# Layer 0 of a graph-attention network: logits with neighbours on partitions, block sums moved behind their transposes, and a new order for the opening turn

## The chip, the cores and the metric

The kernel runs on 1 core of one Trainium2 chip. The metric is the device time of one execution in microseconds (us). Before the change the median of 3 runs is 3023.37 us (3021.89 to 3024.65). TensorE is called PE here, VectorE DVE, ScalarE ACT, GpSimd POOL; SP is the engine that issues all DMAs of this kernel.

## The reference

Two layers work on x of 128 graphs with 64 nodes and 768 features, all in float32. This is layer 0 with its residual and norm, which the change touches (12 heads of 64):

```
h    = einsum('bnd,ade->bane', x, W);  th = tanh(h)
attn = (th @ w_src) + swapaxes(th @ w_dst, 2, 3)        # [b, a, n, m]
attn = where(attn >= 0, attn, 0.2 * attn)
attn = where(~adj, -999.0, attn);  attn = softmax(attn, axis=-1)
f    = elu(einsum('banm,bame->bane', attn, h) + b)
gate = sigmoid(x @ H_w.T + H_b)
x1   = layernorm(x + gate * f + (1 - gate) * x)
```

Layer 1 is a 6-head attention on x1 (q, k, v, an adjacency mask, an output product, residual, norm). Its value product v = x1 @ Wv is computed in the first stage together with layer 0.

## The kernel before

**Tiles.** 64 tiles of 128 tokens (two graphs each) are taken in 32 pairs. A product of a pair (256 x 768 by 768 x 768) is done with seven half-size products instead of eight (Strassen-Winograd), numbered 1 to 7; each is six matmuls 128 x 384. The input side needs four block sums of each operand: `weight_sums` for a weight, `block_sums` for x (`x_sums`, on POOL) and for x1 (`v_sums`, on DVE). A `Job` (L150 to L198) holds the two accumulators of one product, y and z. Products 1, 6, 7 and 4 accumulate in the same y bank, 5 and 3 in the same z bank, so each has to wait until the result before it was read out of the bank (`way_out`).

**Turns.** The first stage is one loop over p (L563), 34 turns. Turn p computes the h and gate products of pair p ("h", "g"), and the attention, norm and value product of pair p-1 ("v", and "u" for the two last v products, which fall into the turn after). `TURN` (L52) is the order of the 21 products in a turn, positions 0 to 20. All other work is hung on these positions by hand, with `at(pos, ...)` (L584 to L614). [...] A product's way out is emitted after the next product (`step`, L208), or at once where the position holds no product (`flush`).

**One tile's attention.** `products` takes tanh of h (ACT) and multiplies by w_dst (DVE) and w_src (POOL); `terms` reduces both (DVE), sends the dst terms to DRAM, waits on SP for their landing, and loads them back spread over partitions as `dd`; `with_bias` adds the bias to h (POOL) and makes `hx`, h with the two graphs of a tile swapped. `logits` adds source and dst terms (DVE), `leaky` applies the slope (ACT), `masked` writes -999 by a predicate, takes the row maximum and subtracts it (DVE), `exps` takes exp (ACT). Now nodes n are on partitions and neighbours m are on the free axis, so `probs_by_nodes` turns the probabilities with six PE transposes per tile, and ACT copies the result `pT` out of PSUM. `attend` multiplies by h (24 matmuls 64 x 64 x 66 on PE, with a column of ones that gives the softmax denominator), `features` divides (DVE) and takes exp for elu (ACT), `elu1`, `gated` (DVE) and `residual` (POOL) form x1, `stats` and `normed` normalise it (DVE, one POOL power, ACT), `by_features` turns it with six PE transposes into `x1T`, which the v product takes. Transposes and attends share two PSUM banks, tag "m" (L95).

In the turn of pair p, `t1`, `t0` are the two tiles of pair p-1 and `n1`, `n0` those of pair p; n1 of one turn is t1 of the next.

**The opening.** All weights are loaded by SP in one row of DMAs, with the sums of w0 and wv on DVE and those of the gate weight on POOL (L262 to L278).

**The second stage** (layer 1, from L629) is not changed, except that a call now reads `all_of(...)`.

Of the kernel before, what the change touches and what calls it, by code (L numbers as in the profile page):

```python
# [9 lines left out]
F32 = mybir.dt.float32  # L10
U8 = mybir.dt.uint8
# [17 lines left out]
NEG0 = -999.0  # L29
# [21 lines left out]

TURN = [  # L52
# [6 lines left out]
def kernel(  # L59
# [4 lines left out]
    adj: bass.AP,  # L64
    w0: bass.AP,
# [36 lines left out]
    dst_d = [dram.tile([P, H0], F32, name=f"dstd_{t}") for t in range(2 * NP)]  # L102
# [10 lines left out]
    neg0 = const.tile([P, 1], F32, name="neg0")  # L113
    V.memset(neg0, NEG0)

# [5 lines left out]
    def load_weight(src, tag, name):  # L121

        w = wpool.tile([P, 7, HK, HALF], F32, tag=tag, name=name)
        view = src.rearrange("(kh kc p) (nh f) -> kh nh p kc f", p=P, kc=HK, nh=2)
        for block, kh, nh in ((B11, 0, 0), (B21, 1, 0), (B22, 1, 1), (T3, 0, 1)):
            nc.sync.dma_start(out=w[:, block], in_=view[kh, nh])
        return w

    def weight_sums(eng, w):
        eng.tensor_tensor(w[:, T1], w[:, T3], w[:, B11], ALU.subtract)  # L130
        eng.tensor_tensor(w[:, T2], w[:, B22], w[:, T1], ALU.subtract)  # L131
        eng.tensor_tensor(w[:, T4], w[:, B21], w[:, T2], ALU.subtract)
        eng.tensor_tensor(w[:, T3], w[:, B22], w[:, T3], ALU.subtract)
# [102 lines left out]
    with ExitStack() as ph:  # L236
# [7 lines left out]
        def load_xT(p):  # L244
            t = sb.tile([P, KC, PAIR * P], F32, tag="xT", name=f"xT_{p}")
            nc.sync.dma_start(out=t, in_=xT[p])
            return t
# [14 lines left out]
        xTs = {0: load_xT(0)}  # L262
# [9 lines left out]
        for s in x_steps:  # L272
            s()
        weight_sums(V, w0_w)
        weight_sums(G, hw_w)
        V.tensor_scalar(b01_bc, b01_bc, 1.0, None, ALU.add)
        wv_w = load_weight(wv, "wc", "wv")
        weight_sums(V, wv_w)  # L278

        def work(name):  # L280
            return sb.tile([P, D], F32, tag="work", name=name, bufs=5)
# [81 lines left out]
        def terms(t):  # L363

            th = st[t].pop("th")
            sd = small.tile([P, 2 * H0], F32, tag="sd", name=f"sd_{t}")
            V.tensor_reduce(sd, th.rearrange("p s (a e) -> p (s a) e", e=E0), AX.X, ALU.add)
            st[t]["sd"] = sd
            nc.sync.dma_start(out=dst_d[t], in_=sd[:, :H0])
            dd = work(f"dd_{t}")  # L370
            for g in range(2):
                nc.sync.dma_start(
                    out=dd[g * N : (g + 1) * N, :],
                    in_=dst_d[t][g * N : (g + 1) * N, :]
                    .rearrange("m a -> (m a)")
                    .partition_broadcast(N),
                )
            st[t]["dd"] = dd

        def with_bias(t):  # L380

            h = st[t]["h"]
            G.tensor_tensor(
                h[:, :, :E0], h[:, :, :E0], b01_bc.unsqueeze(1).to_broadcast([P, H0, E0]), ALU.add
            )

            hx = sb.tile([P, J0, EP], F32, tag="hx", name=f"hx_{t}")
            nc.sync.dma_start(out=hx[:N], in_=h[N:, :J0, :])
            nc.sync.dma_start(out=hx[N:], in_=h[:N, J0:, :])
            st[t]["hx"] = hx  # L390

        def logits(t):
            sd, dd = st[t].pop("sd"), st[t].pop("dd")
            att = work(f"att_{t}")
            att3 = att.rearrange("p (a m) -> p a m", m=N)
            V.tensor_tensor(
                att3,
                dd.rearrange("p (m a) -> p a m", a=H0),
                sd[:, H0:].unsqueeze(2).to_broadcast([P, H0, N]),
                ALU.add,  # L400
            )
            st[t]["att"] = att

        def leaky(t):
            att = st[t]["att"]
            S.activation(att, att, AF.Prelu, alpha=LEAKY)

        def masked(t):

            att = st[t]["att"]  # L410
            att3 = att.rearrange("p (a m) -> p a m", m=N)
            V.copy_predicated(
                att3,
                st[t]["nadj"].unsqueeze(1).to_broadcast([P, H0, N]),
                neg0.unsqueeze(1).to_broadcast([P, H0, N]),
            )
            mx = small.tile([P, H0], F32, tag="mx", name=f"mx_{t}")
            V.tensor_reduce(mx, att3, AX.X, ALU.max)
            V.tensor_tensor(att3, att3, mx.unsqueeze(2).to_broadcast([P, H0, N]), ALU.subtract)

        def exps(t):

            att = st[t].pop("att")
            prob = work(f"prob_{t}")
            S.activation(
                prob.rearrange("p (j a m) -> p a j m", a=2, m=N),
                att.rearrange("p (a j m) -> p a j m", a=2, m=N),
                AF.Exp,
            )
            st[t]["prob"] = prob  # L430
# [8 lines left out]
        def probs_by_nodes(t):  # L439
            prob = st[t].pop("prob")  # L440
            pT = sb.tile([P, J0, P], F32, tag="pT", name=f"pT_{t}", bufs=1)
            for half in range(2):
                transposed(
                    pT[:, 3 * half : 3 * half + 3, :],
                    prob[:, half * HALF : (half + 1) * HALF],
                    f"pTp_{t}_{half}",
                )
            st[t]["pT"] = pT

        def attend(t):  # L450
            pT, h, hx = st[t].pop("pT"), st[t].pop("h"), st[t].pop("hx")
            av = [bank("m", f"av_{t}_{a}") for a in range(2)]
            for j in range(J0):
                for a in range(2):
                    rows = slice(a * N, (a + 1) * N)
                    for g in range(2):
                        T.matmul(
                            av[a][g * N : (g + 1) * N, j * EP : (j + 1) * EP],
                            pT[rows, j, g * N : (g + 1) * N],
                            h[rows, a * J0 + j, :] if a == g else hx[rows, j, :],  # L460
                            start=True,
                            stop=True,
                        )
            st[t]["av"] = av
# [62 lines left out]
        def mask(p):  # L527
            ad = load_adj(sb, 2 * p, PAIR, f"adj_{p}")
            na = sb.tile([P, PAIR, N], U8, tag="nadj", name=f"nadj_{p}", bufs=2)
            V.tensor_scalar(na, ad, 0, None, ALU.is_equal)  # L530
            for i in range(PAIR):
                st[2 * p + i]["nadj"] = na[:, i, :]
# [23 lines left out]
        def x_sums(p):  # L556
            A[p], steps = sums_of(G, "sx", xTs[p], f"x{p}")
            for s in steps:
                s()
# [3 lines left out]
        for p in range(NP + 2):  # L563
# [8 lines left out]
            def at(pos, ok, *acts):  # L572
                if ok:
                    plan.setdefault(pos, []).extend(acts)

            def do(f, *args):
                return lambda: f(*args)
# [4 lines left out]


            at(0, old, do(probs_by_nodes, t1), do(exps, t0), do(gate_tanh, t1))  # L584
            at(1, old, do(residual, t1))
            at(2, old, do(attend, t1), do(gate_tanh, t0))
            at(3, old, do(features, t1), do(probs_by_nodes, t0), do(residual, t0))
            at(4, old, do(elu1, t1), do(gated, t1))
            at(5, old, do(attend, t0), do(stats, t1))
            at(6, old, do(features, t0), do(normed, t1))  # L590
            at(7, old, do(elu1, t0), do(gated, t0))
            at(8, old, do(by_features, t1), do(stats, t0))
            at(9, old, do(normed, t0))
            at(12, old, do(v_begins))
            at(15, old, lambda: v_sums[q][0](), lambda: v_sums[q][1](), do(spill_features, q))
# [8 lines left out]
            at(11, old, do(by_features, t0))  # L604
# [4 lines left out]
            at(16, new, do(logits, n1))  # L609
            at(17, new, do(leaky, n1))  # L610
            at(17, p + 1 < NP, do(x_sums, p + 1))
            at(18, new, do(masked, n1), do(logits, n0))
            at(19, new, do(exps, n1), do(leaky, n0))
            at(20, new, do(masked, n0))  # L614

            for pos, (job, i) in enumerate(TURN):
                ok = {"h": new, "g": new, "v": old, "u": 0 <= p - 2 < NP}[job]
                if ok:
                    step(jobs["u" if job == "u" else job], int(i))
                else:  # L620
                    flush()
                for act in plan.get(pos, ()):
                    act()
# [5 lines left out]
    with ExitStack() as ph:  # L629
# [24 lines left out]
        weight_sums(V, wq_w)  # L654
        loaded = load_group(0)
        wk_w = load_weight(wk, "wb", "wk")
        weight_sums(V, wk_w)
        wf_w = load_weight(wf, "wc", "wf")
        weight_sums(V, wf_w)
# [260 lines left out]
```

## Time and profile before

The profiled execution took 3022.04 us of device time; its span from the first to the last instruction is 3020.0 us, and 2.04 us lie around it.

| what | number |
|---|---|
| median of 3 runs | 3023.37 us |
| profiled execution, its span | 3022.04 us, 3020.0 us |
| mean granted TensorE clock | 0.986 |
| opening until the second turn's first product | 0 to 51.8 us |
| first stage, steady turns | 45.6 us each |
| last product of the first stage ends, layer 1's first starts | 1515 us, 1532.5 us |

In the groups, a line is that of a helper where one records all products (L173). "[idle <- X]" is the time that the engine stood idle before an instruction, and what ended it. "DMA issue" is the time on SP; the landing comes later.

### The profile page before, as it was taken

To read this page: it belongs to the slowest core of one execution; us is meant where nothing else is said; L and a number is where in the kernel's file an instruction comes from. 1 tells how busy PE (TensorE), PEld (TensorE's weight loads), DVE (VectorE), ACT (ScalarE), POOL (GpSimd) and SP (SyncE) were. 2 spreads that over 40 slices of the span, in tenths; PEclk is the share of its full clock that TensorE was granted. 3 is DMA by queue.
4 is the path that set the end of the run, shared out by engine and by line. 5 is a ranking of instruction groups with operands and counts; after the bars stand their busy time and mean duration, and the time that the engine had idled before them with its cause. 6 is when DMAs were issued, how large, how long until landed. Compare 5 with 4: busy or idle time off the path is not lost. (4 is left out here: it accounts for less than half of the span.)

```text
span 3020.0 us, 45321 instructions
## 1 busy us (share of the span) xinstructions
PE 2931.3 (97%) x18048; PEld 2029.7 (67%) x18048; DVE 1830.8 (61%) x3017; ACT 1006.5 (33%) x1761; POOL 805.5 (27%) x650
## 2 busy tenths in 40 slices
PE   6999999999999999999869999999999999999997
PEld 3666666666666666666558777787777787777784
DVE  5888888888888888888633344434344434344434
ACT  2444344344444444444412222222222222222221
POOL 4324324324323333333212111211211211211211
PEclk8999999999999999999879999999999999999998
DMA  4333333333333333333242111222111222111211
GB/s 168 115 112 109 116 118 107 112 120 112 108 121 114 109 117 119 107 113 114 90 146 86 62 57 58 85 85 79 62 57 57 85 85 79 62 57 57 85 64 63
DMA packets 174929, 284.81 MB, mean 94 GB/s; under 512 B 46208, under 2 KB 112768, under 8 KB 174720
## 3 DMA queue, kind: packets, MB, share of 16 engines
q1 hardware_dynamic: 174720, 281.92, 28.7%
q8 instruction: 143, 2.34, 0.3%
q14 instruction: 66, 0.54, 0.1%
HBM read 167.81 MB, written 101.06 MB: 89 GB/s over the span
## 5 line engine op out<-in xcount | busy, mean ns | idle before, releaser
L487 POOL TENSOR_TENSOR x<-gate,x 128x768 f32<-128x768 f32 x64 | 116.5, 1821 | 330.9 <-ACT gate L538 330.9
L780 POOL TENSOR_TENSOR y<-y,bf_bc 128x768 f32<-128x768 f32 x64 | 114.3, 1816 | 301.7 <-DMA y<-x1d 301.7
L804 DVE TENSOR_TENSOR y<-y_o,y 128x384 f32<-128x384 f32 x128 | 69.8, 553 | 178.0 <-PE y_o L173 171.0
L222 POOL TENSOR_TENSOR rs_b<-ve_b,minus_half 128x1 f32<-128x1 f32 x64 | 35.1, 549 | 483.6 <-DVE ve_b L220 480.7
L675 DVE TENSOR_TENSOR kT<-z_k,kT 128x256 f32<-128x256 f32 x96 | 40.5, 422 | 203.6 <-ACT kT L674 108.9
L173 PE MATMUL y_q<-a,wq 128*128 128x256 f32 x576 | 141.7, 382 | 17.4 <-DMA a<-x1Td 17.4
L360 POOL TENSOR_TENSOR th<-th,wsd 128x768 f32<-128x768 f32 x64 | 116.0, 1812 | 157.5 <-DVE th L359 157.5
L143 POOL TENSOR_TENSOR sq_q<-a,a 128x768 f32<-128x768 f32 x16 | 29.5, 1844 | 466.6 <-PE y_o L173 311.0
L674 ACT ACTIVATE qT<-y_q,bq_c 128x256 f32<-128x256 f32 x144 | 67.3, 468 | 244.6 <-PE y_q L173 222.8
L173 PE MATMUL y_k<-a,wk 128*128 128x256 f32 x576 | 144.9, 388 | 1.8 <-DMA wk<-in_wk_dram 1.8
L173 PE MATMUL y_g<-hw,sx_x 128*128 128x384 f32 x384 | 136.0, 491 | 10.5 <-DVE gate L336 10.5
L173 PE MATMUL z_k<-sq_q,wk 128*128 128x256 f32 x576 | 141.5, 382 | 4.1 <-DVE qT L675 4.1
L173 PE MATMUL y_o<-wf,so_o 128*128 128x384 f32 x384 | 134.4, 494 | 8.8 <-DVE y L804 8.8
L173 PE MATMUL y_h<-w,xT 128*128 128x384 f32 x384 | 136.3, 492 | 6.8 <-DMA w<-in_w_dram 6.8
L173 PE MATMUL y_k<-sq_q,wk 128*128 128x256 f32 x576 | 141.5, 382 | 0.7 <-DVE wk L131 0.7
L173 PE MATMUL y_q<-sq_q,wq 128*128 128x256 f32 x576 | 140.0, 379 | 0.0
L173 PE MATMUL z_q<-sq_q,wq 128*128 128x256 f32 x576 | 140.0, 379 | 0.0
L222 POOL TENSOR_TENSOR rs_a<-ve_a,minus_half 128x1 f32<-128x1 f32 x64 | 35.2, 551 | 383.9 <-DVE ve_a L220 383.9
L173 PE MATMUL z_v<-wv,sv_v 128*128 128x384 f32 x384 | 137.5, 495 | 0.1
L173 PE MATMUL z_h<-w,sx_x 128*128 128x384 f32 x384 | 137.6, 495 | 0.0
L173 PE MATMUL y_h<-w,sx_x 128*128 128x384 f32 x384 | 135.5, 490 | 1.7 <-DVE w L131 1.7
L173 PE MATMUL y_v<-wv,x1T 128*128 128x384 f32 x384 | 136.5, 492 | 0.6 <-ACT v L349 0.6
(163 smaller groups left out, 6718.7 us busy)
## 6 DMA issues: line engine op xcount, KB each, us to landing
xT<-in_xT_dram SPq DMA_DIRECT2D x32, 768.0 KB, 7.0
x<-in_x_dram SPq DMA_DIRECT2D x64, 384.0 KB, 3.5
dd<-dstd SPq DMA_DIRECT2D x128, 192.0 KB, 3.4
x1d<-x SPq DMA_DIRECT2D x64, 384.0 KB, 2.5
x1Td<-x1T SPq DMA_DIRECT2D x32, 768.0 KB, 4.8
vd<-v SPq DMA_DIRECT2D x64, 384.0 KB, 2.9
a<-x1Td SPq DMA_DIRECT2D x64, 384.0 KB, 3.3
v<-vd SPq DMA_DIRECT2D x384, 64.0 KB, 2.3
```

The source lines that it names most:

```text
L143: lambda: eng.tensor_tensor(s1, a21, a22, ALU.add),
L173: T.matmul(to[:, : self.n], lhsT, rhs, start=kc == 0 and not more, stop=kc == HK - 1, skip_group_check=more,)
L222: G.tensor_tensor(rstd, ve, minus_half, ALU.pow)
L360: G.tensor_tensor(th[:, 1, :], th[:, 1, :], wsd[:, 1, :], ALU.mult)
L487: G.tensor_tensor(xp, st[t]["gate"], xp, ALU.mult)
L674: lambda mn, bk_: S.activation(at(*mn), bk_, AF.Identity, bias=bias(mn[1])),
L675: lambda mn, bk_: V.tensor_tensor(at(*mn), bk_, at(*mn), ALU.add),
L780: G.tensor_tensor(y[:, i, :], y[:, i, :], bf_bc, ALU.add)
L804: V.tensor_tensor(at(*mn), b, at(*mn), ALU.add)
```

## The change

It has five parts.

1. **Logits transposed.** The source terms, not the dst terms, go through DRAM and come back as `ss`, spread so that a partition is a neighbour m and the free axis is (n, head). The own term of the second half of the heads has to come from the tile's other graph, which two small DMAs bring (`dx`). The mask becomes a cap, `cap` (-300 for no edge, 1e30 for an edge), on a transposed copy of the adjacency that the host prepares (`adjT`), and the logits take the minimum with it. The row maximum and its subtraction go. `exps` writes `pT` directly, with a step of 64 elements. `probs_by_nodes` goes, with its 12 transposes a turn and the copies of ACT.
2. **Positions.** `attend` and everything after it moves one to three positions earlier, the logits of n1 and n0 one later (17, 19), `gate_tanh` and `residual` of the first tile into the turn before (19, 20).
3. **x1 sums.** `by_features` of t0 moves from 11 to 10; the first two `v_sums` from 15 to 11, ahead of `products`.
4. **The opening.** Turn 0 runs all h products, then all gate products (`FIRST`), with every way out at once. A weight's third block to load is now T3, then B22. The sums of wv are spread over turn 1.
5. **Small.** `work` has 4 buffers for 5, `pT` 2 for 1; the bias's +1 goes to POOL; the first xT is loaded in two parts.

```diff
-NEG0 = -999.0
+NEG0 = -300.0
+BIG = 1e30
+FIRST = ["h1", "h2", "h6", "h5", "h7", "h4", "h3", "g1", "g2", "g6", "g5", "g7", "g4", "g3"]
+FIRST_AT = {11: 7, 12: 8, 13: 9, 14: 10, 15: 11, 17: 12, 18: 13, 19: 13, 20: 13}
...
-        for block, kh, nh in ((B11, 0, 0), (B21, 1, 0), (B22, 1, 1), (T3, 0, 1)):
+        for block, kh, nh in ((B11, 0, 0), (B21, 1, 0), (T3, 0, 1), (B22, 1, 1)):
...
-        V.tensor_scalar(b01_bc, b01_bc, 1.0, None, ALU.add)
+        G.tensor_scalar(b01_bc, b01_bc, 1.0, None, ALU.add)
         wv_w = load_weight(wv, "wc", "wv")
-        weight_sums(V, wv_w)
...
-            nc.sync.dma_start(out=dst_d[t], in_=sd[:, :H0])
-            dd = work(f"dd_{t}")
-            for g in range(2):
...
+            nc.sync.dma_start(
+                out=src_d[t].rearrange("(a g) (n j) -> (g n) a j", a=2, j=J0),
+                in_=sd[:, H0:].rearrange("p (a j) -> p a j", j=J0),
+            )
+            ss = work(f"ss_{t}")
+            for r in range(2):
+                rows = src_d[t][0:4:3, :] if r == 0 else src_d[t][1:3, :]
+                nc.sync.dma_start(
+                    out=ss[r * N : (r + 1) * N, :].rearrange("p (a x) -> p a x", a=2),
+                    in_=rows.partition_broadcast(N),
+                )
+            dx = small.tile([P, J0], F32, tag="dx", name=f"dx_{t}")
+            nc.sync.dma_start(out=dx[:N], in_=sd[N:, J0:H0])
+            nc.sync.dma_start(out=dx[N:], in_=sd[:N, J0:H0])
...
-            V.tensor_tensor(
-                att3,
-                dd.rearrange("p (m a) -> p a m", a=H0),
...
+            for a, d in ((0, sd[:, :J0]), (1, dx)):
+                half = slice(a * HALF, (a + 1) * HALF)
+                V.tensor_tensor(
+                    att[:, half].rearrange("p (n j) -> p n j", j=J0),
+                    ss[:, half].rearrange("p (n j) -> p n j", j=J0),
+                    d.unsqueeze(1).to_broadcast([P, N, J0]),
+                    ALU.add,
+                )
             V.tensor_tensor(
+                att.rearrange("p (x j) -> p x j", j=J0),
+                att.rearrange("p (x j) -> p x j", j=J0),
+                st[t]["cap"].unsqueeze(2).to_broadcast([P, 2 * N, J0]),
+                ALU.min,
             )
...
-            V.copy_predicated(
...
-            V.tensor_reduce(mx, att3, AX.X, ALU.max)
-            V.tensor_tensor(att3, att3, mx.unsqueeze(2).to_broadcast([P, H0, N]), ALU.subtract)
...
+        def probs(t):
             S.activation(att, att, AF.Prelu, alpha=LEAKY)
+            pT = sb.tile([P, 2, J0, N], F32, tag="pT", name=f"pT_{t}")
             S.activation(
+                pT.rearrange("p a j n -> p a n j"),
+                att.rearrange("p (a n j) -> p a n j", a=2, j=J0),
                 AF.Exp,
             )
...
-        def probs_by_nodes(t):
...
             for j in range(J0):
                 for a in range(2):
                     for g in range(2):
+                        r = g if a == 0 else 1 - g
+                        rows = slice(r * N, (r + 1) * N)
...
-                            pT[rows, j, g * N : (g + 1) * N],
-                            h[rows, a * J0 + j, :] if a == g else hx[rows, j, :],
+                            pT[rows, a, j, :],
+                            h[rows, j, :] if a == 0 else hx[rows, j, :],
...
+            cap = sb.tile([P, PAIR, 2 * N], F32, tag="cap", name=f"cap_{p}")
+            V.tensor_scalar(cap, ad, BIG, NEG0, ALU.mult, ALU.add)
...
-            at(0, old, do(probs_by_nodes, t1), do(exps, t0), do(gate_tanh, t1))
-            at(1, old, do(residual, t1))
-            at(2, old, do(attend, t1), do(gate_tanh, t0))
-            at(3, old, do(features, t1), do(probs_by_nodes, t0), do(residual, t0))
-            at(4, old, do(elu1, t1), do(gated, t1))
-            at(5, old, do(attend, t0), do(stats, t1))
-            at(6, old, do(features, t0), do(normed, t1))
-            at(7, old, do(elu1, t0), do(gated, t0))
-            at(8, old, do(by_features, t1), do(stats, t0))
-            at(9, old, do(normed, t0))
-            at(12, old, do(v_begins))
-            at(15, old, lambda: v_sums[q][0](), lambda: v_sums[q][1](), do(spill_features, q))
+            at(0, old, do(probs, t0), do(gate_tanh, t0))
+            at(1, old, do(residual, t0))
+            at(1, old, do(attend, t1))
+            at(2, old, do(features, t1))
+            at(3, old, do(attend, t0), do(elu1, t1), do(gated, t1))
+            at(4, old, do(features, t0), do(stats, t1))
+            at(5, old, do(elu1, t0), do(gated, t0))
+            at(6, old, do(normed, t1), do(stats, t0))
+            at(8, old, do(by_features, t1), do(normed, t0))
+            at(10, old, do(by_features, t0))
+            at(11, old, do(v_begins), lambda: v_sums[q][0](), lambda: v_sums[q][1]())
+            at(15, old, do(spill_features, q))
...
-            at(11, old, do(by_features, t0))
...
-            at(16, new, do(logits, n1))
-            at(17, new, do(leaky, n1))
+            at(17, new, do(logits, n1))
             at(17, p + 1 < NP, do(x_sums, p + 1))
-            at(18, new, do(masked, n1), do(logits, n0))
-            at(19, new, do(exps, n1), do(leaky, n0))
-            at(20, new, do(masked, n0))
+            at(18, new, do(probs, n1))
+            at(19, new, do(logits, n0), do(gate_tanh, n1))
+            at(20, new, do(residual, n1))
...
+            if p == 1:
+                for pos, s in zip((0, 2, 4, 6), weight_sums(V, wv_w)):
+                    at(pos, True, s)
+            for pos, (job, i) in enumerate(TURN if p > 0 else FIRST):
...
```

## The prediction

> **What bounds the kernel now.** I read first the engines' shares and the slices by time, then three steady turns by window, then the order in time of one turn, and last who waits for whom in the steady part.
>
> ```profile
> PE   6999999999999999999869999999999999999997
> DVE  5888888888888888888633344434344434344434
> PEclk8999999999999999999879999999999999999998
> ```
> The first 19 slices (75.5 us each) are the first stage. PE is full there but for the first slice.
>
> ```profile
> 790.40:836.00 45.60, 45.60 (x248) 27.71 (x247) 37.91 (x55) 19.94 (x33) 16.52 (x14) 1.00 0.35 113
> 836.00:881.60 45.60, 45.60 (x248) 27.72 (x247) 37.90 (x55) 19.93 (x33) 16.52 (x14) 1.00 0.36 117
> ```
> The columns are the window, then busy PE, weight loads, DVE, ACT, POOL, the clock, DMA. A turn is 45.60 us of PE with no gap; DVE has 37.9. So PE work that goes is time saved, until something else comes late.
>
> ```profile
> 835.98 2.10 PE L173 MATMUL y_h<-w,xT 128*128 128x384 f32 x6
> 837.91 0.82 PE L436 MATMUL pTp<-ident,prob 128*128 128x128 f32 x6
> 838.57 2.10 PE L173 MATMUL x_h<-w,xT 128*128 128x384 f32 x6
> ```
> A product takes 1.936 us from start to start, this group of six transposes 838.57 - 837.91 = 0.66; the other, behind an attend, 0.78 (in the last full turn, 1438.20 to the next product at 1438.98). Together 1.44 us a turn.
>
> What comes next behind PE is the turn's own latency:
>
> ```profile
> 809.36 1.01 ACT L226 ACTIVATE x<-x,sh_a,rs_a 128x768 f32<-128x768 f32 x1
> 811.37 0.82 PE L436 MATMUL x1Tp<-ident,x 128*128 128x128 f32 x6
> ```
> x1 of t1 is normed at 810.37, and PE turns it at 811.37: 1.0 us in hand. That is less than the 1.44 the change takes from PE.
>
> **What the Trainium skill says.** "TensorE: Matmul & The Clock Gate", section PE-mode transpose, gives about 275 ns for a transpose in a kernel; the trace has the same mean (280), but queued behind each other six take 0.66 us, 0.11 each, so the sum uses that. "SBUF — State Buffer", section Who interferes with whom: a DVE instruction with two SBUF inputs and a POOL instruction that reads SBUF lock each other out for a whole instruction. The trace agrees for the lock, on a tensor-scalar, which the page also names:
>
> ```profile
> 845.44 1.82 POOL L487 TENSOR_TENSOR x<-gate,x 128x768 f32<-128x768 f32 x1 [0.16 <-ACT gate L538]
> 845.64 1.70 DVE L530 TENSOR_SCALAR nadj<-adj 128x128 uint8<-128x128 uint8 x1
> ```
> The mask took 0.21 us at 34.1 alone, here 1.70, until POOL ended. The same page, section Door 1: The DMA port swizzle, has a penalty for steps beyond 16 bytes; the logits' add, which reads `dd` at 48 bytes, has a least time of 1.52 us against 0.96 for other adds of that size, which agrees. "DMA: Bandwidth & Descriptors", Specifications, says that pieces under 512 B cost a read-modify-write; the dst terms (48 B pieces) landed after 1.4 us at least, and no row separates this.
>
> **The change, part by part.** *Transposes*: 2 x 6 a turn, minus 1.44 us of PE, if nothing comes late; the four ACT copies behind them (0.48 us each) go too, off the path. The attend's 24 matmuls keep number and size, and their order still alternates quadrants: 0. *DVE per tile*: out go 1.89 (add), 1.09 (predicated copy), 0.95 (max), 0.96 (subtraction); in come two adds of 384 (0.56 each by rows of that size) and a minimum of 768 (0.96): 2.0 us from start to end. DVE drops by about 2 x 2.8 = 5.6 to 32 us of a 44.2 us turn, so it is no bound by busy time. The mask doubles its elements: 0.2 to 0.3 us.
>
> *The chain of waits of a turn.* I time from T, the end of product h4 (815.90 here). E, the start of the next turn, is T + 20.1 before and after.
> - Terms of n1. Before, the dst DMA is issued at 822.85, T + 6.95. `by_features` t0 now stands ahead of it: on ACT two copies (0.86) come ahead of the copy of h4 and the tanh, and the second tanh product waits for POOL's lock. I get +1.1: T + 8.0. The two sums themselves are not what is waited for (the first needs only t1, the second the first copy of t0).
> - SP. In order it has src n1, ss, ss, dx, dx, hx, hx, src n0, ss, ss, dx, dx. From the rows of before: landing of the terms 1.45 (824.30 - 822.85), taken as 1.65 for twice the pieces (1.45 to 2.0); from first load to next store 2.48 (826.78 - 824.30), plus two dx issues at 0.56 = 3.6; landing of n0's terms 2.95 before, behind 0.6 MB of loads, now 1.7 because the dx issues let these drain (1.5 to 2.95); second ss issue 0.55; its landing 3.5 (dd: 3.1 to 3.8). Sum 11.0 (10.6 to 12.2): the data of n0 are there at T + 19.0, or E - 1.1.
> - Logits n0: 2.0, to E + 0.95. Then `probs` (0.87 + 0.75), tanh of the gate (1.6) and the copy of h1 on ACT, on which DVE waits with h2's add, and the features queue behind that add (before: 42 us of such waits in 17 turns, 2.5 each): 4.25. Features of t1 start at E + 5.2; before, 844.25 - 835.98 = 8.27. They also free the two PSUM banks that the attend of t0 needs, at E + 6.7; PE comes to it at E + 8.7 (four products and an attend), so that costs 0, and would cost from features at E + 7.2 on.
> - From there to the normed x1: before 855.96 - 844.25 = 11.7. Now `elu1`, `gated` of t0 (3.0) stand ahead of the shift of t1, less the mask's lock, which is gone: 13.8. Ready at E + 19.0.
> - PE wants it at E + 21.0 - 1.44 = E + 19.55. In hand: 0.5 us.
>
> So a turn becomes 45.60 - 1.44 = 44.16, at a small margin. I book 0.15 us a turn for stalls: thirty turns (2 to 31) give 30 x (1.44 - 0.15) = 38.7 us.
>
> *Exp with a step of 256 bytes on ACT*: not in the trace. Below, 0.84 as now; above, about 1.5 (twice per element). A gain is excluded, because the element count stays. I take 0.84; the top would use up the margin (+0.1 to +0.6 a turn, 3 to 18 us).
>
> *Opening.* Before, DVE waits for wv (27.3) and sums until 33.6, with the gate's first add behind, and PE starts g6 at 34.93. Now the wv sums are gone from there, but the mask at position 3 is on DVE behind a load that landed at 29.4 (issued 19.8, 9.6 to landing), behind wv in the queue. Behind the mask stands h7's add, and h3 needs that bank: h3 starts near 30.4, at a cold clock (+1.6, as g6 has now: 3.68 against 2.10). Then seven gate products and a wait for g7's add: turn 1 begins at 48.5 (before 51.79). Its logits of n0 have data at 53.4, minimum done at 56.2, features at 60.6, x1T at 75.9 against 81.82 now. The wv sums add 2.7 there, included. Gain 6 us (1 to 10). w0's blocks in the new order bring h6 forward by 1.4, which the mask hides.
>
> *Close.* After the last full turn v1 starts 1498.52 - 1474.26 = 24.3 us later. By the same steps without h: logits E + 0.95, tanh done 4.2, elu t1 6, gated t0 14.5, norm 18, turned and copied 19.9. Gain 4 us (1.5 to 4.5). The 17.4 us of load wait ahead of layer 1 stay, and layer 1 stays.
>
> Sum against the profiled 3022.0: -38.7 -6 -4 = 2973.3. The median of before is 1.3 above its profiled execution: 2974.6, so 2975.
>
> **Rivals.**
> *R1, slower: DMA and POOL's lock make the turn's latency the bound.* `residual` of n1 is on POOL at position 20, after probs n1 and tanh n1. By my sums it would start at T + 20.3 (n1's data at 13.7, logits 2.0, lock waits with `x_sums` 1.1, ACT 3.4), 1.8 us long. If the data of n0 come 1.3 us later than I hold, it runs first, and logits n0 end at 20.3 + 1.8 + 2.0 = T + 24.1, E + 4.0. Norm is then ready 3.05 later, 2.5 after PE wants it: 46.67 a turn. 30 x 1.07 - 6 - 1.5 (close) = +24.5, 3048; with the exp at its top, 3066. It costs more than is saved from a stall of 1.7 us a turn (1.44 and 7.5/30), that is logits n0 after E + 3.2. For it: the margin is 0.5 on a sum of ten terms. Against: DVE has 12 us free, and SP's rings drain.
> *R2, between: POOL slips in between adds and minimum.* Logits end at 20.3 + 1.8 + 0.96 = E + 2.95; stall 1.45; the turn stays at 45.6. -6 -1.5: 3014.5, and with its scatter 2998 to 3022.
> *R3: the margin is larger and PE has no stall*: 3022.0 - 43.2 - 10 = 2968.8, 2970 as a median. It is the lower part of my forecast.
> That the transposes were hidden anyway is excluded by 45.60 of 45.60.
>
> **How the numbers follow.** My forecast with R3 (2958 to 2988) has 0.50, R2 0.22, R1 0.24 (3030 to 3066), and 0.04 is left for an end near 3023. A measurement of this kernel tells 0.2% (6 us) from no change. Faster by more: all of the first and most of R2, 0.70. Within: the rest of R2 and the left-over, 0.07. Slower 0.23. The range goes from 2958 to 3040, which takes in R2 and the lower part of R1 and leaves out less than 0.2.
>
> **What would show it.** Steady turns of 44.2 us with PE busy throughout show the main step right. `x1Tp` on PE with a wait on the norm (ACT L226's successor) of 1 to 3 us in each turn shows R1 or R2; then see whether logits n0 starts beside POOL's residual or behind a DMA. The opening is wrong if DVE's mask doesn't wait near 29 us, or PE doesn't stall at h3. An exp of more than 1 us shows the step's price. I am wrong in kind if attends take more than 0.9 us, or if a turn is long with no wait at `x1Tp`.

## The result and the profile after

The changed kernel takes 3060.68 us (median of 4 runs, 3059.68 to 3065.31) against 3023.02 for the kernel before (4 runs, 3021.89 to 3024.65): ratio 1.0127, 95% interval 1.011 to 1.0145. It is slower by 38 us, where 2975 was forecast. The profiled execution is the longest of the four, 3065.31 us with a span of 3063.4, so its trace shows about 5 us more loss than the median has.

The slices by time, of the kernel after:

```profile
PE   6999999999999999999959999999999999999997
...
DVE  4666666766667666666643434343443433443434
...
PEclk8999999999999999999979999999999999999998
```

A nine hides up to a tenth, so PE's row doesn't show the loss: the first stage is only longer, and so is each slice (76.6 us against 75.5). DVE is mostly at 6 where it was at 8, as forecast. Two windows in the steady part show the loss (busy PE, weight loads, DVE, ACT, POOL, clock, DMA share, GB/s):

```profile
400.00:800.00 400.00, 382.15 (x1943) 227.39 (x1942) 270.93 (x447) 164.26 (x236) 141.10 (x117) 0.99 0.34 110
800.00:1200.00 400.00, 384.44 (x1985) 229.10 (x1984) 267.66 (x433) 167.77 (x238) 147.20 (x122) 0.99 0.35 111
```

PE was busy for the whole of every window before; now it stands idle for 33.4 us in 800, 2.0 in a turn. The first x1 transpose comes at 78.99 and that of the thirtieth turn after it at 1498.02: 47.30 us a turn against 45.60. The account of the span, against the 3020.0 of before:

| stretch | forecast | measured |
|---|---|---|
| opening, to the first x1 transpose | -6 | 78.99 - 81.82 = -2.8 |
| thirty turns | -38.7 | 1419.0 - 1367.9 = +51.1 |
| last full turn's x1 transpose to v1 | -4 | 48.67 - 48.80 = -0.1 |
| v1 to layer 1's first product | 0 | -0.8 |
| layer 1 | 0 | 1483.6 - 1487.5 = -3.9 |
| sum | -48.7 | +43.5 |

Who waits in PE's steady part (engine, line waited for, us in total, times, longest):

```profile
PE av L457 <- DVE rden L473: 17.4, 16, 1.8
...
PE y_h L185 <- ACT h L332: 6.4, 12, 0.5
...
PE x1Tp L446 <- ACT x L238: 4.6, 12, 0.4
```

The wait that the forecast had watched, the x1 transpose on the norm, is the smallest. The large one is the second attend of a turn: its PSUM banks are still being read by the features of the first (L473). But that is where a late chain becomes visible, not where it is late. The chain of waits that ended last tells the loop. These are pieces of it in one turn, the ones that matter below and all of its PE products (start, us, what):

```profile
466.44 1.33 DVE th L371
467.77 1.68 DVE sd L379
469.47 2.17 DMA srcd<-sd
...
475.60 2.38 DMA srcd<-sd
...
478.66 3.35 DMA ss<-srcd
...
482.58 2.17 DVE att L417
...
486.64 1.53 ACT pT L435
...
494.03 0.97 DVE ex L497
...
504.95 1.94 PE y_g L185 x6
506.89 1.94 PE y_h L185 x6
```

Only two products are left in it, those between the two x1 transposes: the other products wait for the attention chain, and that chain for two round trips of the source terms through DRAM, one for each tile.

Now a turn read with the prediction's letters, T = 840.13 (end of h4's product) and E = 860.14 (start of the next turn). It is one of the longest, 48.17 us; medians over all turns stand in the part on why the prediction was wrong. The DMA issues of SP, then DVE and POOL at the logits of n0:

```profile
848.17 0.38 SPq L382 DMA_DIRECT2D srcd<-sd  x1
850.77 1.28 SPq L389 DMA_DIRECT2D ss<-srcd  x2
852.11 0.59 SPq L394 DMA_DIRECT2D dx<-sd  x1
852.74 0.59 SPq L395 DMA_DIRECT2D dx<-sd  x1
853.44 0.53 SPq L406 DMA_DIRECT2D hx<-h  x1
854.02 0.59 SPq L407 DMA_DIRECT2D hx<-h  x1
854.71 0.53 SPq L382 DMA_DIRECT2D srcd<-sd  x1
857.48 1.27 SPq L389 DMA_DIRECT2D ss<-srcd  x2
```
```profile
861.31 1.81 POOL L487 TENSOR_TENSOR x<-gate,x 128x768 f32<-128x768 f32 x1 [3.18 <-ACT gate L542]
...
861.64 1.89 DVE L417 TENSOR_TENSOR att<-ss,sd 128x384 f32<-128x384 f32 x1 [3.09 <-DMA ss<-srcd]
...
863.46 0.55 DVE L417 TENSOR_TENSOR att<-ss,dx 128x384 f32<-128x384 f32 x1
...
864.04 0.96 DVE L423 TENSOR_TENSOR att<-att,cap 128x768 f32<-128x768 f32 x1
```

The rows stand in the order of the program: SP issues `ss` once `src` has landed, 2.60 us (850.77 - 848.17) and 2.77 (857.48 - 854.71) after it, and the second `src` only behind the loads of n1. DVE's first add takes 1.89 where its twin takes 0.55: POOL began its residual 0.33 earlier, and the add ended 0.41 after POOL was done (863.12). In what follows, "the lock" is this wait of DVE for POOL. Then PE, at the second attend:

```profile
867.00 2.10 PE L185 MATMUL z_v<-wv,sv_v 128*128 128x384 f32 x6
...
870.75 0.33 PE L457 MATMUL av<-h,pT 64*64 64x66 f32 x4 [1.65 <-DVE rden L473]
...
872.25 3.86 PE L185 MATMUL y_h<-w,sx_x 128*128 128x384 f32 x6
875.90 2.17 PE L185 MATMUL y_g<-hw,xT 128*128 128x384 f32 x6
```

From z_v's end (868.94) to the next product lie 3.31 us, where an attend with nothing in its way takes 0.95: 2.36 lost. Then that product itself takes 3.65 to the next start, where it is 2.04 after other attends: 1.61 more at half the clock. In the trace's record of the clock it is granted half from 872.64 to 876.05. Together 3.97 of the 4.0 by which this turn is longer than 44.15, the 45.60 of before less the 1.44 of the transposes.

### The profile page after: what moved, and what is told of

It is laid out like the page before. It is cut to its first block, busy times and chain, and to the rows that moved or that the text cites. A ratio compares the mean times of both kernels' runs of the same rounds, so it can differ in the third digit from the quotient of the medians.

```text
span 3063.4 us, 44395 instructions
## 1 busy us (share of the span) xinstructions
PE 2912.2 (95%) x17664; PEld 1999.3 (65%) x17664; DVE 1638.4 (53%) x2951; ACT 996.4 (33%) x1633; POOL 821.5 (27%) x651
## 4 chain that ended last, share of the span: by engine, by line
PE 56%; DVE 15%; DMA 8%; ACT 8%; POOL 6%; issue 3%; SPq 3%; DVEq 0%; ACTq 0%; POOLq 0%
PE y_k L185 8%; PE y_o L185 8%; PE y_q L185 8%; PE z_o L185 4%; PE z_k L185 4%; PE z_q L185 4%; DMA ss<-srcd 4%; PE y_h L185 4%; DMA srcd<-sd 3%; PE y_g L185 3%; POOL th L372 2%; POOL h L401 2%; PE x_k L185 2%; PE x_o L185 2%; PE x_q L185 2%
## 5 line engine op out<-in xcount | busy, mean ns | idle before, releaser
L185 PE MATMUL y_h<-w,sx_x 128*128 128x384 f32 x384 | 152.4, 537 | 11.7 <-ACT h L332 11.7
L185 PE MATMUL y_q<-a,wq 128*128 128x256 f32 x576 | 141.4, 382 | 17.6 <-issue 17.6
L234 POOL TENSOR_TENSOR rs_a<-ve_a,minus_half 128x1 f32<-128x1 f32 x64 | 57.3, 895 | 370.7 <-DVE ve_a L232 370.7
L185 PE MATMUL y_g<-hw,xT 128*128 128x384 f32 x384 | 135.5, 489 | 0.7 <-DVE gate L348 0.7
```

Of the source, the lines that this page charges most:

```text
L185: T.matmul(to[:, : self.n], lhsT, rhs, start=kc == 0 and not more, stop=kc == HK - 1, skip_group_check=more,)
L234: G.tensor_tensor(rstd, ve, minus_half, ALU.pow)
```

## The experiments

Theory A: the transposes did leave PE, and 44.15 us of products, attends and x1 transposes a turn would be the bound; but the chain of latencies, terms through DRAM, logits, attend, features, norm, is now longer than that. Theory B: something in the new form itself costs what it saves (the strided exp, the attend's banks, POOL), and no order of the same work would bring it back. All edits are made to the kernel after, except the last one. Ratios are to runs of the kernel before on the same chip, whose medians are 3022.51 (experiments 1 to 4), 3023.2 (5, 6, 8, 9) and 3021.46 (7). A turn's length is the mean of thirty, from first x1 transpose to first x1 transpose.

**1. POOL's residual of n1 back to where it was**, at entry 1 of the next turn, with the tanh of the gate: it no longer stands on POOL when the logits of n0 arrive.

```diff
-at(0, old, do(probs, t0), do(gate_tanh, t0))
-at(1, old, do(residual, t0))
+at(0, old, do(probs, t0), do(gate_tanh, t1))
+at(1, old, do(residual, t1))
...
-at(2, old, do(features, t1))
-at(3, old, do(attend, t0), do(elu1, t1), do(gated, t1))
+at(2, old, do(gate_tanh, t0), do(features, t1))
+at(3, old, do(residual, t0), do(attend, t0), do(elu1, t1), do(gated, t1))
...
-at(19, new, do(logits, n0), do(gate_tanh, n1))
-at(20, new, do(residual, n1))
+at(19, new, do(logits, n0))
```

> The gate's tanh and POOL's residual of the first tile go back to where they stood before the change (positions 0 and 1 of the next turn, those of the second tile 2 and 3), so that POOL no longer holds the shared port when the logits of n0 begin. Theory A, one loop of latency round the turn in which every link counts: the lock costs 1.48 us (DVE's first add is recorded from 861.64 and goes on when POOL ends at 863.12), so a turn falls from 47.3 to about 45.9 and the time from 3061 to about 3018. Rival B, the data of n0 come late and the lock only lies beside that wait: no change, 3061 (within 6). Rival C, what counts is DVE's wait for the x1 sums behind the transposes: no change either.

Measured 3032.51 us, ratio 1.0033 (1.002 to 1.0045), turns 46.11. Of the 128 adds of the logits, those that took over 1.0 us fell from 35 to 11, and the logits of n0 take 2.02 us in the median turn where they took 3.53: the lock is gone from them, and 28 us with it. That is less than the 43 expected. The data of n0 come as late here (T + 20.6 in the median) as in the kernel after (20.7), and that lateness still has its cost without the lock.

**2. The exp written in order**, so that the attend reads its weights in steps instead.

```diff
-pT = sb.tile([P, 2, J0, N], F32, tag="pT", name=f"pT_{t}")
+pT = sb.tile([P, 2, N, J0], F32, tag="pT", name=f"pT_{t}")
 S.activation(
-    pT.rearrange("p a j n -> p a n j"),
+    pT,
...
-    pT[rows, a, j, :],
+    pT[rows, a, :, j],
```

> The exp writes its result in the order in which it reads (n, then head), and the attend takes its stationary operand with a step of 24 bytes. Theory A: the exp falls from 1.54 to 0.85 us, which is on the path for n0, and the first tile's exp makes POOL's residual 0.7 earlier, which takes as much from the lock: 0.7 to 1.4 us a turn, 3061 to 3019 to 3040. Against it stands the attend: if PE loads weights slower at that step, each of its 48 loads a turn takes longer; with loads twice as long that is up to 2 x 0.9 us a turn and the time stays at 3061 or rises to 3075. Rivals B and C: the exp is not waited for, no gain.

Measured 3034.21 us, ratio 1.0039 (1.0024 to 1.0054), turns 46.24. The groups of this kernel, then of after, in 400 to 1200 us (busy, mean ns, idle before):

```profile
L435 ACT ACTIVATE pT<-att 128x768 f32<-128x768 f32 x34 | 28.7, 843 | 1.1
...
L457 PE MATMUL av<-h,pT 64*64 64x66 f32 x816 | 54.8, 279 | 0.4 <-DVE rden L473 0.4
...
L457 PEld LDWEIGHTS av<-hx,pT 64*64 64x64 f32 x816 | 49.9, 204 | 0.5 <-issue 0.3
```
```profile
L435 ACT ACTIVATE pT<-att 128x768 f32<-128x768 f32 x34 | 52.3, 1539 | 1.1
...
L457 PE MATMUL av<-h,pT 64*64 64x66 f32 x792 | 34.4, 226 | 17.4 <-DVE rden L473 17.4
...
L457 PEld LDWEIGHTS av<-hx,pT 64*64 64x64 f32 x792 | 26.9, 136 | 6.8 <-issue 6.8
```

The step of 256 bytes costs ACT 0.70 us per exp (1539 - 843 ns). The step of 24 bytes makes a weight load 204 ns instead of 136, and an attend of 24 matmuls longer by 24 x (54.8/816 - 33.1/864) = 0.69, where 33.1 us for 864 is the same group with nothing in its way, in the kernel of experiment 5. Wherever the step is put, about the same is paid. Here the short exp wins 26 us, which theory A, latency as the bound, explains: the exp is in the chain and the weight loads are not.

**3. `hx` of n1 behind the terms of n0** on SP: two issues fewer ahead of the second `src`.

```diff
-at(13, new, do(terms, n1), do(with_bias, n1))
-at(14, new, do(terms, n0), do(with_bias, n0))
+at(13, new, do(terms, n1))
+at(14, new, do(terms, n0), do(with_bias, n1), do(with_bias, n0))
```

> The bias step of n1 with its two hx loads goes behind the terms of n0, so that SP issues the terms of n0 1.2 us earlier. Theory A: the data of n0 land at about 860.4 on the scale of the profiled turn, two adds start ahead of POOL's residual (861.3), the minimum waits for it; logits n0 end 0.9 earlier, a turn falls to 46.4 and the time to about 3034. Rival B (the landing alone): the whole 1.2 us, 3025. Rival C: no change, 3061.

Measured 2988.71 us, ratio 0.9889 (0.9875 to 0.9904), far under all three expected times; turns 44.85 in the mean, so 2.4 a turn from data that come 1.3 earlier (T + 19.4 in the median). Two turns of this kernel show why it is more than the 1.3, the one long, the other short:

```profile
731.70 2.13 POOL L487 TENSOR_TENSOR x<-gate,x 128x768 f32<-128x768 f32 x1 [3.18 <-ACT gate L542]
...
732.20 2.44 DVE L423 TENSOR_TENSOR att<-att,cap 128x768 f32<-128x768 f32 x1
```
```profile
822.73 2.64 POOL L487 TENSOR_TENSOR x<-gate,x 128x768 f32<-128x768 f32 x1 [3.18 <-ACT gate L542]
...
822.73 0.96 DVE L423 TENSOR_TENSOR att<-att,cap 128x768 f32<-128x768 f32 x1
```

POOL's residual takes 1.81 alone. In the second pair DVE's minimum takes its usual 0.96 and it is POOL that waits, which nothing on the critical path feels; in the first POOL is ahead and DVE waits 1.5. Nearly all turns are 44.1 to 44.9 or 45.6 to 46.8: 1.3 us decide who is first, and 1.5 to 1.8 hang on that.

**4. The second tile's steps and the x1 sums at their positions of before.** The attend of t0 goes from 3 to 5, and everything of t0 behind it moves with it, so that elu and gate product of t0 no longer stand ahead of the norm of t1 on DVE.

```diff
-at(3, old, do(attend, t0), do(elu1, t1), do(gated, t1))
-at(4, old, do(features, t0), do(stats, t1))
-at(5, old, do(elu1, t0), do(gated, t0))
-at(6, old, do(normed, t1), do(stats, t0))
-at(8, old, do(by_features, t1), do(normed, t0))
-at(10, old, do(by_features, t0))
-at(11, old, do(v_begins), lambda: v_sums[q][0](), lambda: v_sums[q][1]())
+at(3, old, do(elu1, t1), do(gated, t1))
+at(4, old, do(stats, t1))
+at(5, old, do(attend, t0))
+at(6, old, do(features, t0), do(normed, t1))
+at(7, old, do(elu1, t0), do(gated, t0))
+at(8, old, do(by_features, t1), do(stats, t0))
+at(9, old, do(normed, t0))
...
+at(11, old, do(by_features, t0))
+at(12, old, do(v_begins))
+at(15, old, lambda: v_sums[q][0](), lambda: v_sums[q][1](), do(spill_features, q))
```

> Attend, features, elu, gate, norm and transposes of the second tile and the x1 sums go back to the positions of before the change (attend at 5, transposes at 11, sums at 15); logits, caps, probabilities, the gate's tanh and residual and the opening stay as changed. Theory A: PE no longer stands at the second attend for banks that the first tile's features free (2.4 us and a cold product), the shift of t1 has 3 us less ahead of it, and the terms of n1 are 1.1 earlier; x1 of t1 is ready at most 0.5 us after PE wants it, a turn is 44.2 to 44.9, the time 2970 to 2990. Rival B: the data of n0 still come late and everything hangs on them: 45.5 or more, above 3005. Rival C: the sums were the cause: the gain is the 1.1 us of their place, 46.2, 3027.

Measured 2986.81 us, ratio 0.9881 (0.9867 to 0.9896), turns 44.76. PE's wait at the attend is gone from the list; the longest left is this:

```profile
PE y_v L185 <- DVE sv_v L156: 6.8, 13, 0.7
```

Two of the change's own moves, attend and tail of t0 earlier and x1 sums earlier, thus cost 74 us in this kernel, more than all the transposes save. How much of that is the banks, how much the order on DVE, and how much the terms of n1, which now go out at T + 7.4 in the median and not at T + 8.0, this run doesn't separate.

**5. Edits 1, 3 and 4 together**, and **6. the same with edit 2.** ("Residual back to one turn entry earlier" in the expectation is edit 1.)

> The kernel after with three edits of its order together: residual back to one turn entry earlier, hx of layer n1 later so that the source terms are issued first, and the second tile's steps at their positions of before. Theory A (the turn's chain of latencies was the bound and each edit shortens it): the matmul work becomes the bound again, turns near 44.15 us, 2965 to 2975 us. Rival (another wait takes over, PSUM banks or POOL): not under 2985 us, no better than the best of the single edits.

> The three edits of order together, and the exponential written in order, with the attend matmuls' weights read in steps in its place. Theory A: once the matmul work is the bound, the 0.7 us that ACT saves is worth nothing and the slower weight loads cost 0.68 us per attend, 1.36 us a turn, about 41 us in all: near 3010 us. Rival (the exponential's 1.54 us still sets the end of the turn): at or under the time of the three edits alone.

Measured 2970.46 us, ratio 0.9826 (0.9813 to 0.984), and 3010.89, ratio 0.9958 (0.9943 to 0.9973). The windows, first of the three edits, then with the exp in order:

```profile
400.00:800.00 400.00, 400.00 (x2116) 239.86 (x2115) 292.99 (x472) 181.03 (x254) 151.44 (x129) 1.00 0.38 118
```
```profile
400.00:800.00 400.00, 400.00 (x2074) 244.88 (x2074) 282.21 (x454) 163.96 (x246) 148.23 (x125) 1.00 0.37 114
```

PE is full again in both. Turns are 44.19 in the first and 45.54 in the second (44.15 and 45.50 but for the first turn of each); the difference, 1.35, is near twice the 0.69 of experiment 2, which is due in each of the two attends of a turn. The same edit that won 26 us when latency was the bound loses 40 when PE is: theory A, and B is out, since the same work in another order is 90 us faster than the kernel after. It is also where the prediction's R3, a turn with no stall, had put the change: 2970.

**7. Which of the three are needed.** Each pair of edits 1, 3 and 4:

> Two of the three edits of order: hx of layer n1 behind the source terms of n0, and the second tile's steps where they were before; POOL's residual of n1 stays at entry 20. Theory A (the three shorten one and the same chain, so their gains do not add: whatever takes the chain under the 44.15 us of matmul work is enough): 2968 to 2975 us. Rival (POOL's residual still gets in ahead of the minimum in some turns and holds the end of those turns up): 2978 to 2987 us.

> Two of the three edits of order: hx of layer n1 behind the source terms of n0, and POOL's residual of n1 where it was before; the first tile's elu and gate product stay ahead of the second tile's norm. Theory A: with the shared port free the turns of 46.3 us that the edit of hx alone still had are gone, 2968 to 2977 us. Rival (the residual, moved to the next turn, puts the norm of the second tile later, and the early steps of the other tile stand before it): 2985 to 3000 us.

> Two of the three edits of order: the second tile's steps and POOL's residual of n1 where they were before; the source terms of n0 are still sent behind hx of n1. Theory A: 2968 to 2977 us, since the chain has the 2.5 us or more that the other two give and needs no more. Rival (the terms of n0 come 1.3 us too late for what is left of the turn): 2980 to 2995 us.

| edits | median (range) us | ratio to before, 95% | turn |
|---|---|---|---|
| 3 and 4 | 2968.79 (2966.69 to 2970.8) | 0.9824 (0.981 to 0.9839) | 44.24 |
| 1 and 3 | 2996.07 (2993.7 to 2999.09) | 0.9915 (0.9901 to 0.993) | 44.94 |
| 1 and 4 | 2976.01 (2975.64 to 2977.03) | 0.9849 (0.9832 to 0.9865) | 44.28 |

Alone the edits win 28, 72 and 74 us; together they win 90, not 174. That is one chain with a floor under it. Edit 4 is in both pairs that come near the floor. For edits 1 and 3 the rival's number was right: turns are 44.1 to 46.3, much as with edit 3 alone (44.1 to 46.8), and edit 1 gains nothing there (2996.07 against 2988.71). Whether its reason, a later norm of the second tile, is the right one was not tested. The first pair, `hx` behind the terms, t0 late, and the residual where the change put it, does with two edits what all three do; the 1.7 us between them lie within their ranges.

**8. The terms in fewer pieces.**

```diff
-out=src_d[t].rearrange("(a g) (n j) -> (g n) a j", a=2, j=J0),
-in_=sd[:, H0:].rearrange("p (a j) -> p a j", j=J0),
+out=src_d[t].rearrange("r (q c) -> (r q) c", c=H0),
+in_=sd[:, H0:],
```

> The kernel after, with the source terms written to DRAM as 128 contiguous pieces of 48 B in place of 256 of 24 B; the rows are then in another order than the read expects, so the logits take the terms of wrong rows, and only the time is read. Theory A (number and size of the pieces set the landing of 2.6 to 2.8 us): the landing of the terms falls to 1.5 to 1.8 us, the data of layer n0's logits reach DVE about 2 us earlier, turns of 44.2 to 45.4 us, 2975 to 3005 us. Rival (the landing does not depend on the pieces): 2.6 us as before, 3061 us.

Measured 3016.15 us, ratio 0.9983 (0.9973 to 0.9993), turns 45.83. The DMA view from 200 to 1400 us (count, KB, median us to landing), of this kernel, of after, and of before, which sends the dst terms in 128 pieces of 48 B but has the two `hx` loads just ahead of the second store:

```profile
srcd<-sd SPq DMA_DIRECT2D x52, 6.0 KB, 1.6
```
```profile
srcd<-sd SPq DMA_DIRECT2D x50, 6.0 KB, 2.3
```
```profile
dstd<-sd SPq DMA_DIRECT2D x52, 6.0 KB, 2.0
```

The same 6 KB land in 1.6 us as 128 pieces of 48 B and in 2.3 as 256 of 24 B. Number, size and places of the pieces change together here, and the run doesn't tell them apart. In one turn (T = 859.45) `ss` is issued 1.46 and 1.81 after `src`, and the data of n0 are at DVE at 879.16 = T + 19.7, which is also the median; in the kernel after the median is T + 20.7. So the pieces are 1.0 us of the 1.7 by which T + 19.0 was missed. And the turn is not 44.2:

```profile
880.12 1.81 POOL L487 TENSOR_TENSOR x<-gate,x 128x768 f32<-128x768 f32 x1 [3.17 <-ACT gate L542]
...
880.22 2.52 DVE L423 TENSOR_TENSOR att<-att,cap 128x768 f32<-128x768 f32 x1
```

Now POOL slips in between the adds and the minimum, as in the prediction's R2, which gave 3014.5. The landing is thus about half of the loss, 45 us of the 92 that lie between the kernel after and the best order; the 2975 to 3005 expected left the lock out and was missed.

**9. The opening alone**, part 4 of the change in the kernel before (`FIRST`, `FIRST_AT`, T3 ahead of B22, the sums of wv in turn 1, the +1 on POOL, the first xT in two parts; position 16, where before has logits, goes to 12).

> The kernel before, with the change of the opening turn alone (h ahead of the gate, the weight sums spread through turn 1, x in two parts). By the trace of after the first x1 transpose of turn 1 comes 2.8 us earlier, and nothing else moves: 3017 to 3026 us, within 0.2 per cent of before or barely under it. Rival (the opening gives the 6 us that the prediction counted): under 3017 us.

Measured 3020.02 us, ratio 0.9991 (0.9985 to 0.9998): about 3 us, within what was expected, and half of what the prediction counted. But the trace doesn't show them where the expectation put them. Turn 1 begins at 50.04 us, 1.75 earlier than before (51.79), yet its first x1 transpose comes at 82.24, 0.42 later than before (81.82), and layer 1 begins at 1533.55 against 1532.45. What this execution gained, 1.3 us of span, lies in layer 1. So the opening alone doesn't bring the first x1 transpose forward: the 2.8 us in the kernel after came only together with the other parts of the change, and where the 3 us of the medians lie stays open.

## Why the prediction was wrong

The mechanism that took the forecast's place, a chain of latencies longer than PE's work, lengthened by the lock, was on record as R1 (3048; 3066 with the exp at its top), with 0.24. What failed is the sum of the chain. Step by step, in the turn shown above and as the median of 29 turns:

| step, as predicted | forecast | turn shown | median |
|---|---|---|---|
| `src` of n1 issued | T + 8.0 | T + 8.04 | T + 8.04 |
| landing of n1's terms | 1.65 | 2.60 | 1.99 |
| from first load to next store | 3.6 | 3.94 | 3.93 |
| landing of n0's terms | 1.7 | 2.77 | 2.48 |
| second issue and landing of `ss` | 4.05 | 4.16 | 4.27 |
| data of n0 at DVE | T + 19.0 | T + 21.5 | T + 20.7 |
| logits n0 | 2.0 | 3.4, of it 1.3 behind POOL | 3.5 |
| exp, tanh, copy, to the features | 4.25 | 4.8 | 4.8 |
| features of t1 | E + 5.2 | E + 9.7 | E + 9.1 |

So the features of t1 come 3.9 us late in the median turn, against a margin of 0.5: 1.7 from SP's steps, 1.5 from the lock, 0.6 from the exp.

- **The failing step is what twice the pieces cost.** "Landing of the terms 1.45, taken as 1.65 for twice the pieces" allowed 0.2 for the doubling on n1's terms, and the 1.7 for n0's allowed nothing. With 128 pieces (experiment 8) the two landings are 1.45 and 1.74 in the median, as the prediction had them without that price; with 256 they are 1.99 and 2.48. So the argument that the dx issues let the queue drain held, and the doubling cost 0.5 and 0.7. The other 0.6 of SP's 1.7 are in the steps between and after. It is the first step that failed and not the only one: with 128 pieces the kernel still takes 3016 and not 2975, for the exp was taken at its lower bound and the lock at nothing. The spread was too narrow as well: the sum was given as 10.6 to 12.2, while the bounds of its own terms add up to 10.2 and 12.9; the median came out at 12.7. "DMA: Bandwidth & Descriptors", Specifications, names a cost for pieces below 512 B; both sizes here lie below it, so no run tests that limit.
- **The lock.** R1 was to hold "if the data of n0 come 1.3 us later than I hold". They came 1.7 later in the median. In the turn shown POOL started at T + 21.2 (20.3 forecast); logits n0 ended at T + 24.3 in the median (R1: 24.1). So the rival's price was right and its condition likelier than 0.24: with a margin of 0.5 on a sum whose own bounds were 1.6 wide, even chances would have been fair. "SBUF — State Buffer", Who interferes with whom, says that issue order decides who blocks; experiment 3 shows both orders.
- **The place of the stall.** R1 looked for waits of 1 to 3 us at the x1 transpose, and the prediction called itself wrong in kind if a turn were long with no wait there. There the wait is 0.4 at most. PE stalls at the second attend, whose banks were priced at 0. That R1's 3048 and 3066 enclose 3061 is therefore in part luck.
- **Exp.** Bound 0.84 to 1.5, taken at 0.84, measured 1.54. The next ACT instruction starts 1.34 after the start of the exp (865.90 to 867.24), where others of that size give 0.87 (867.24 to 868.11): 0.5 of latency each. The upper bound was right, the choice wrong.
- **Banks.** "Costs 0, and would cost from features at E + 7.2 on" was right as a condition: features at E + 9.7 cost 2.4. That PE in some turns then runs its next product at half clock was not foreseen.
- **Right**: transposes at 1.44 us (turns of 44.15 where nothing is late); from the features to the normed x1 13.5 us in the turn shown (13.8 forecast); DVE at about 32 a turn (31.65 in the turn shown); the mask at 0.29 and h3 at 30.95 (30.4 forecast) in the opening.
- **Opening and close.** Turn 1 begins at 50.19 (48.5), and its first x1 transpose comes at 78.99 (75.9); with the three edits of experiment 5 it comes at 75.70, so what was missing there is largely the same lateness. The close gained 0.1 of the forecast's 4, by the same reading, which was not tested by itself.

The layer 1 term is explained in part. Of its 3.9 us, 3.5 lie in its first 30 us. There the granted clock was 0.69 before and 0.82 after in the first 17.6 us, 0.72 and 1.00 in the next 12.4. And layer 1 is not quite unchanged: it loads its weights by the same helper, so their third and fourth block change places there too. One execution of each kernel doesn't tell the two apart.

## What to carry to other kernels

When work is taken from a full engine, the latency loop behind it has to be summed against the new, shorter turn, and if the margin is smaller than the spread of the sum, the loop is the likely bound. In such a sum the pieces of a small transfer need a price of their own (here 6 KB landed 0.7 us later in twice the pieces), and two engines that lock each other out are a step whose size depends on which comes first, so a microsecond there can be worth more than itself (here 1.3 us of earlier data gave 2.4 a turn). The same edit (here the order in which exp writes) can win or lose by the bound it meets; decide which bound it is first.

## What was not expected of the hardware

- Between full-size products lie 1.8 to 3.8 us at the second attend. In 7 of 29 turns the next product then takes 3.2 to 3.7 to the following start, not 2.04; the stretch ahead of it was 2.9 to 3.8 us there, and up to 3.19 in turns without a drop. So the length of the stretch alone doesn't decide. In each of the seven the trace has the clock at half for 3.41 us, and all these drops start whole multiples of 3.413 us apart (from the first, at 681.49, to 872.64: 56; to 1439.25: 222). Counted in windows of that length, PE was busy for 1.3 to 1.9 us in the one that ends at each drop, and for 1.6 us or more in every other window of the steady turns: it was not idle there, only about half busy or less, and the attend's small matmuls are up to 1.25 us of that. "TensorE: Matmul & The Clock Gate", Part 1: The HAM clock gate, gives an idle window of about 3.4 us whose place is not tied to the kernel's. This trace agrees on length and place; by it, a window with 1.3 to 1.9 us of work in it can count as idle.
- An exp that writes 768 values in steps of 256 bytes: 1.54 us against 0.84 in order. Weight loads of 64 x 64 in steps of 24 bytes: 204 ns against 136.
